# Attention with a routed expert layer on one core: the scatters of a routed group made a job of their own

## The chip, the cores and the metric

The kernel runs on one core of one Trainium2 chip. The metric is the device time of one execution in microseconds (us), median of several runs. Five engines work side by side, each through its own queue of instructions: TensorE (PE in the profile; its weight loads are PEld), VectorE (DVE), ScalarE (ACT), GpSimd (POOL) and SyncE (SP, which here only starts transfers).

## The reference

Everything is float32. `x` has 8 batches of 1024 tokens of 256 values.

```python
def attn(x, Wq, Wk, Wv, Wo):                 # 16 heads of 16
    q, k, v = (einsum('oi,bsi->bso', W, x) split into heads)
    score = where(causal, q @ k.T / 4, -inf)
    return einsum('oi,bsi->bso', Wo, softmax(score) @ v)

def ffn(h, router_weight, router_bias, gate_up_proj, gate_up_bias, down_proj, down_bias):
    scores = softmax(h @ router_weight.T + router_bias)      # 8 experts
    topk_w, topk_idx = top_k(scores, 2)
    gu = h @ gate_up_proj[e] + gate_up_bias[e]               # for every expert e, 2 * 512 wide
    gate, up = minimum(gu[:512], 7), clip(gu[512:], -7, 7)
    down = ((up + 1) * gate * sigmoid(1.702 * gate)) @ down_proj[e] + down_bias[e]
    return sum of the two chosen experts' down, weighted by topk_w

x = x + layernorm(attn(layernorm(x)))
x = x + layernorm(ffn(layernorm(x)))
```

Only the two chosen experts of a token need to be computed. The kernel therefore sorts the tokens by expert on the chip.

## The kernel before, in words

**Two phases.** First attention and routing, then the experts. Between them lies a DRAM buffer `xsd`: one region of rows for each expert, into which every token's normalized row is scattered twice, once for each chosen expert.

**Attention.** The work is cut into 32 units: 8 batches by 4 sets of four heads. A unit has nine steps, and each step has two halves ("half steps", one for each pair of heads), 18 half steps for a unit. While unit u takes its row maxima (matmuls `sa`, L834, reduced on DVE), unit u-1 makes its exponentials and weighted values (matmuls `sb`, L929, exponentials on ACT, L941, causal masks on POOL, L950, matmuls `av`, L970). After the last unit comes one more pass, u = 32, with only the second half of this work.

**Groups and their routing.** Two chunks of 512 tokens leave each batch, 16 "groups" in all, t = 0 to 15. A group's job (`finish`, then `route`) does, one after another: the output projection (matmuls `yps`, L1031), a layer norm and the residual on POOL (L517 the power, L529 the normalization, L1050 the sum), a second layer norm into `xn` (L529 again), four transposes by two (`x2ps`, L1092), the router's logits (`lpsT` L1099, `lps` L1107), softmax and ranks on DVE (L1109 to L1149), a count of the tokens of each expert (`cps`, L1153) and from it each token's row in `xsd` (`slots`). At its end stand eight indirect DMAs of POOL, the scatters of L1194: 128 rows of 258 values each. `finish` of group t waits until group t-2 has transposed its `xn`, and goes on to `route` only when the whole job of group t-2 is done.

**Tables.** After group 11 and after group 15 the job goes on into `table` (L308 to L438 and further): from the counts it works out which expert and which rows each tile of 256 tokens takes. The table after group 11 serves the first 16 tiles. Four tiles' rows are loaded at once by `load_early` (L1283, on SP); these loads read `xsd`, so they have to follow the scatters of groups 0 to 11 both in the program and on the chip.

**Who sets the order.** PE, DVE, ACT and SP execute in the order in which the program was written down. That order is made by a small planner while the kernel is being built. Each job is a generator that yields `piece(pe, dve, act, pool, after)`: the cost of its next piece on each engine and the number of half steps that must pass first. A half step adds its spare time to a credit of each engine (`earn`, at most 0.9 us, POOL 1.3 us). `pump` then takes every piece whose engines have credit left, in the order urgent jobs, the first `due` job, `back` jobs from oldest to newest, and counts one half step. On POOL the order follows the same source order (`in_order`), except that scatters may change places among each other. Where something must be finished, the planner emits pieces without asking for credit: at the end of unit 31 it did so with the oldest `back` job until the table after group 11 stood:

```python
if u == B * NG - 1 and not early:
    while NT - LATE not in known:
        emit(back, back[0])
    load_early()
```

**Experts.** 72 tiles at most, in the order of the tables; `quarter` (matmuls `gu`, L1470), `lower_half` (matmuls `dn`, L1510), an indirect DMA of the results to `ytd` (L1523), and `both`, which adds the two results of each token. The jobs of groups 12 to 15 are carried on beside the first tiles; before tile 14 whatever is left of them is emitted at once (`finish_all`).

## Time and profile before

| | |
|---|---|
| three runs | 2163.42, 2168.82, 2172.29 us, median 2168.82 |
| profiled execution | 2165.1 us, span on the core 2163.0 us |
| busy PE, DVE, ACT, POOL | 2053.6, 1711.3, 1062.6, 1053.1 us |
| the 128 scatters of L1194 on POOL | 129.0 us, mean 1008 ns |
| attention | from the start to about 1380 us of the span |
| experts | from about 1380 us to the end |

PE is busy for 95% of the span. A busy PE share says little about how much it could save, so what is read below is what stands between its matmuls: for each stretch, the time in which PE did nothing, and the instruction of another engine whose end let it go on. In a line of the timeline the columns are the start, the duration, the engine, the line of the kernel, the operation with output and input, and in brackets the idle time of the engine before it with what ended it.

### The profile page before, as it was taken

What the parts mean: (1) busy time and instruction counts of PE and PEld (TensorE: products, weight loads), DVE (VectorE), ACT (ScalarE), POOL (GpSimd) and SP (SyncE); (2) the same over time, 40 slices, a digit from 0 to 9 for tenths busy, and PEclk for the clock granted to TensorE, in tenths of its full rate; (3) what the DMA queues carried; (4) which work ended last, traced back from release to release, by engine and by line L of the source; (5) the groups of instructions that cost most, each with busy time, mean ns of one, the idle gap of its engine ahead of it and who ended that gap; (6) DMA issues with size and microseconds to landing.
All of it is one profiled execution on the core that took longest, in us unless ns stands there. A gap on an engine that the chain in (4) does not pass through costs nothing.

```text
span 2163.0 us, 44648 instructions
## 1 busy us (share of the span) xinstructions
PE 2053.6 (95%) x16205; PEld 1260.0 (58%) x16205; DVE 1711.3 (79%) x4091; ACT 1062.6 (49%) x2072; POOL 1053.1 (49%) x1213
## 2 busy tenths in 40 slices
PE   7899999999999999999999998999999999999995
PEld 3444444444444434434534443688888888888884
DVE  4786886986887887887888788678777888877776
ACT  3566665666666655655655665533123222232222
POOL 3421653472474355455554645455544444444443
PEclk9999999999999999999999999999999999999998
DMA  4101102112112111112111111656877777766774
GB/s 124 24 16 43 35 26 63 34 45 46 42 32 69 20 45 46 49 45 50 47 37 41 44 39 36 209 198 210 263 248 250 268 271 264 261 241 239 271 273 152
DMA packets 147096, 254.85 MB, mean 118 GB/s; under 512 B 21504, under 2 KB 106008, under 8 KB 144952
## 3 DMA queue, kind: packets, MB, share of 16 engines
q1 hardware_dynamic: 133128, 217.01, 32.5%
q0 software_dynamic: 12528, 34.36, 4.3%
q8 instruction: 129, 2.11, 0.4%
q14 instruction: 95, 0.78, 0.1%
q10 hardware_dynamic: 1216, 0.58, 0.1%
HBM read 171.13 MB, written 55.63 MB: 105 GB/s over the span
## 4 chain that ended last, share of the span: by engine, by line
PE 68%; DVE 19%; POOL 6%; issue 4%; ACT 2%; DMA 1%; DVEq 0%; ACTq 0%; POOLq 0%; SPq 0%
PE sa L834 18%; PE gu L1470 14%; PE av L970 10%; PE dn L1510 7%; PE sb L929 5%; PE yps L1031 3%; PE pjk L740 3%; PE pjq L740 3%; PE vps L726 3%; DVE mx L850 3%; DVE sa L844 2%; DVE acc L1585 1%; DVE gate L1479 1%; DVE act L1491 1%; DVE up L1483 1%
## 5 line engine op out<-in xcount | busy, mean ns | idle before, releaser
L941 ACT ACTIVATE pT<-sb 128x512 f32<-128x512 f32 x1134 | 616.3, 595 | 392.3 <-PE sb L929 356.4
L929 PE MATMUL sb<-qP,kP 32*128 32x512 f32 (+3 forms) x3072 | 701.0, 525 | 13.8 <-ACT pT L941 8.9
L834 PE MATMUL sa<-kP,qP 32*128 32x512 f32 (+3 forms) x3072 | 653.7, 525 | 26.0 <-DVE mx L844 13.4
L1470 PE MATMUL gu<-xsT,wg 128*128 128x256 f32 (+1 forms) x2208 | 485.2, 372 | 1.9 <-ACT xsT L1450 1.9
L1470 PEld LDWEIGHTS gu<-xsT,wg 128*128 128x128 f32 x2208 | 407.5, 190 | 56.1 <-ACT xsT L1450 3.4
L850 DVE TENSOR_REDUCE mx<-sa 128x2 f32<-128x1024 f32 x256 | 310.6, 1215 | 116.9 <-PE sb L929 89.7
L950 POOL TENSOR_SCALAR_AFFINE_SELECT pT<-pT 128x512 f32<-128x512 f32 x256 | 164.1, 656 | 466.4 <-ACT pT L941 455.5
L834 PEld LDWEIGHTS sa<-kP,qP 32*128 32x128 f32 x3072 | 226.3, 185 | 248.8 <-issue 100.0
L1481 ACT ACTIVATE sig<-gate 128x256 f32<-128x256 f32 (+1 forms) x276 | 112.8, 409 | 523.9 <-DVE gate L1479 488.2
L970 PE MATMUL av<-pT,vpad 128*32 128x256 f32 (+1 forms) x5120 | 350.2, 370 | 5.0 <-DVE avs L981 3.0
L929 PEld LDWEIGHTS sb<-qP,kP 32*128 32x128 f32 x3072 | 294.1, 185 | 47.1 <-ACT pT L941 18.1
L1486 POOL TENSOR_TENSOR sig<-sig,gate 128x256 f32<-128x256 f32 (+1 forms) x276 | 198.7, 723 | 248.4 <-ACT sig L1481 245.4
L970 PEld LDWEIGHTS av<-pT,vpad 128*32 128x32 f32 x5120 | 117.0, 109 | 292.7 <-issue 235.1
L1510 PE MATMUL dn<-wd,act 128*128 128x256 f32 x1064 | 259.6, 383 | 18.0 <-DVE act L1491 16.8
L1510 PEld LDWEIGHTS dn<-wd,act 128*128 128x128 f32 x1064 | 194.2, 190 | 51.9 <-DVE act L1491 28.7
L1479 DVE TENSOR_SCALAR gate<-gu,bs 128x256 f32<-128x256 f32 (+1 forms) x276 | 128.9, 467 | 106.2 <-PE gu L1470 94.0
L844 DVE CUSTOM_DVE_ANT_0 sa<-sa,cmask 128x512 f32<-128x512 f32 x256 | 177.6, 698 | 39.7 <-PE sb L929 20.3
L1523 POOL DMA_INDIRECT ytd<-ys,places x133 | 133.4, 1003 | 125.2 <-DVE ys L1518 92.7
L1194 POOL DMA_INDIRECT xsd<-xn,slots x128 | 129.0, 1008 | 63.7 <-DVE xn L1190 34.3
L1491 DVE SCALAR_TENSOR_TENSOR act<-up,sig 128x256 f32<-128x256 f32 (+1 forms) x276 | 124.5, 451 | 26.6 <-POOL sig L1486 26.6
L869 ACT COPY edge<-sa 128x512 f32<-128x512 f32 x192 | 112.9, 588 | 41.2 <-DVE mx L859 20.2
L888 DVE TENSOR_REDUCE mx<-edge 128x8 f32<-128x1024 f32 x96 | 115.6, 1205 | 18.1 <-POOL edge L883 18.1
(243 smaller groups left out, 2335.0 us busy)
## 6 DMA issues: line engine op xcount, KB each, us to landing
wg<-_L_ffn_gate_up_proj_dram SPq DMA_DIRECT2D x69, 1024.0 KB
wd<-in_L_ffn_down_proj_dram SPq DMA_DIRECT2D x69, 512.0 KB
xs<-xsd SPq DMA_DIRECT2D x60, 258.0 KB
yy<-ytd SPq DMA_DIRECT2D x15, 1024.0 KB
bs<-biasd SPq DMA_DIRECT2D x69, 132.0 KB
x<-in_L_attn_x_dram SPq DMA_DIRECT2D x16, 512.0 KB
aT<-avn SPq DMA_DIRECT2D x256, 32.0 KB
x1d<-y SPq DMA_DIRECT2D x16, 512.0 KB
```

The costliest lines, as they stand in the source:

```text
L834: nc.tensor.matmul(ps[:, hh, ds(at, w)], lhsT=qP[r, ts(i, P)], rhs=kP[r, ds(c * QC, w)], start=True, stop=True,)
L844: nc.vector.tensor_tensor_reduce(out=ps[:, hh, :], in0=ps[:, hh, :], in1=cmask, scale=1.0, scalar=NEG, op0=ALU.add, op1=ALU.max, accum_out ...
L850: nc.vector.tensor_reduce(mx[:, heads, i, 2:3], ps, AX.X, ALU.max)
L929: nc.tensor.matmul(banks[hh][:, ds(at, QC - off)], lhsT=kP[r, ts(j, P)], rhs=qP[r, ds(c * QC + off, QC - off)], start=True, stop=True,)
L941: nc.scalar.activation(pT[:, 2 * pair + hh, :], banks[hh], AF.Exp)
L950: in_order(nc.gpsimd.affine_select(out=d, in_=d, compare_op=ALU.is_ge, fill=0.0, base=0, pattern=[[0, HG], [1, P]], channel_multiplier=-1,))
L970: nc.tensor.matmul(av[ds(hh * HS, HS), ds(off + a - at, z - a)], lhsT=vp[:, j, ds((g * HG + hh) * VS, HS)], rhs=pT[:, hh, a:z],  start=c n ...
L1470: nc.tensor.matmul(ps[:, half, :w], lhsT=wg[:, kt, ds(half * FF + f * P, P)], rhs=xT[:, kt, :], start=(kt == 0), stop=(kt == KT - 1),)
L1479: nc.vector.tensor_scalar(gt, ps[:, 0, :w], bs[:, f : f + 1], LIMIT, ALU.add, ALU.min)
L1486: in_order(nc.gpsimd.tensor_tensor(sg, sg, gt, ALU.mult))
L1491: nc.vector.scalar_tensor_tensor(act[:, f, :w], up, 1.0 - LIMIT, sg, ALU.max, ALU.mult)
L1510: nc.tensor.matmul(pss[n][:, 0, :], lhsT=act[:, f, ts(n, P)], rhs=wd[:, f, :], start=(f == 0), stop=(f == FT - 1),)
```

## The change

The eight scatters at the end of `route` become a generator of their own, `scatter_rows`. For groups 0 to 14 it is started as a new `back` job, with 3 half steps before its first scatter and 4 before each further one, where there was 1 before. For the last group it is run through on the spot. The job of a group then goes on at once to its end, or to its table. Two waits are added: `route` of group t first waits until every scatter of group t-2 has been emitted, since `xn` has two buffers, and the early loads wait until the scatters of groups 0 to 11 have been emitted (`early_known`). At the end of unit 31 the planner now emits one piece of every `back` job in turn, until both the table after group 11 and all those scatters stand.

```diff
+        def scatter_rows(t, xn, last):
+
+            rest = 0 if last else 4
+            for r in range(TOPK):
+                for n in range(NTB):
+                    yield piece(pool=1.1, after=rest if n or r else 1 if last else 3)
+                    put = nc.gpsimd.indirect_dma_start(
...
+        def scattered(t):
+            return t in puts and (t >= NT - TN or puts[t].done)
+
         def route(t, x1, last):
 
+            while t > 1 and not scattered(t - 2):
+                yield piece(after=1)
             xn = ap2.tile([P, NTB, XD], F32, tag="xn2", name=f"xn2_{t}")
...
-            for r in range(TOPK):
-                for n in range(NTB):
-                    yield piece(pool=1.1, after=0 if last and (n or r) else 1)
-                    put = nc.gpsimd.indirect_dma_start(
...
+            puts[t] = scatter_rows(t, xn, last)
+            if last:
+                yield from puts[t]
+            else:
+                puts[t] = start(back, puts[t])
...
+        def early_known():
+            return NT - LATE in known and all(scattered(t) for t in range(NT - LATE))
...
-                    if u == B * NG - 1 and not early and NT - LATE in known:
+                    if u == B * NG - 1 and not early and early_known():
                         load_early()
...
                 if u == B * NG - 1 and not early:
-                    while NT - LATE not in known:
-                        emit(back, back[0])
+                    while not early_known():
+                        for job in list(back):
+                            emit(back, job)
                     load_early()
```

More of the change, by code (lines that the diff above doesn't have):

```diff
@@ L1072, in normed @@
             yield piece(after=1)
+        puts = {}
+        def scatter_rows(t, xn, last):
[4 more added lines that the diff above has]
+                    put = nc.gpsimd.indirect_dma_start(
+                        out=xs_dram[:, :],
+                        out_offset=bass.IndirectOffsetOnAxis(ap=slots[:, t, r, n : n + 1], axis=0),
+                        in_=xn[:, n, :], in_offset=None,
+                    )
+                    in_order(put, scatter=True)
+                    apart(put, "xs")
+        def scattered(t):
+            return t in puts and (t >= NT - TN or puts[t].done)
         def route(t, x1, last):
+            while t > 1 and not scattered(t - 2):
+                yield piece(after=1)
             xn = ap2.tile([P, NTB, XD], F32, tag="xn2", name=f"xn2_{t}")
@@ L1190, in route @@
             nc.vector.tensor_reduce(xn[:, :, D + 1], first_of, AX.X, ALU.add)
-            for r in range(TOPK):
-                for n in range(NTB):
-                    yield piece(pool=1.1, after=0 if last and (n or r) else 1)
-                    put = nc.gpsimd.indirect_dma_start(
-                        out=xs_dram[:, :],
-                        out_offset=bass.IndirectOffsetOnAxis(ap=slots[:, t, r, n : n + 1], axis=0),
-                        in_=xn[:, n, :], in_offset=None,
-                    )
-                    in_order(put, scatter=True)
-                    apart(put, "xs")
+            puts[t] = scatter_rows(t, xn, last)
[3 more added lines that the diff above has]
+                puts[t] = start(back, puts[t])
             if nth == NT - 1:
```

## The prediction

> **What bounds the kernel now.** I read the page's head with the engines' shares first, then the busy time by stretch (start and end, length, then busy us and count of PE, PEld, DVE, ACT and POOL, granted clock, DMA share, GB/s), then PE's timeline where attention ends.

> ```profile
> span 2163.0 us, 44648 instructions
> PE 2053.6 (95%) x16205; PEld 1260.0 (58%) x16205; DVE 1711.3 (79%) x4091; ACT 1062.6 (49%) x2072; POOL 1053.1 (49%) x1213
> ```

> ```profile
> 100.00:1300.00 1200.00, 1160.93 (x11248) 546.62 (x11244) 975.99 (x2177) 745.47 (x1395) 588.42 (x647) 0.99 0.17 42
> 1345.00:1357.00 12.00, 7.68 (x51) 3.12 (x47) 5.22 (x23) 3.46 (x7) 3.90 (x5) 0.73 0.22 52
> ```

> PE sets the time. From 100 to 1300 us it is idle for only 1200 - 1160.93 = 39.1 us. The one place where it waits for long is the end of unit 31, where the granted clock falls to 0.73:

> ```profile
> 1300.99 0.38 PE L1153 MATMUL cps<-chosen,before 128*128 128x32 f32 x2 [2.35 <-DVE chosen L1149]
> ...
> 1346.32 0.64 PE L970 MATMUL av<-pT,vpad 128*32 128x256 f32 x8
> 1346.89 0.39 PE L371 MATMUL firstps<-seg,before 128*128 128x2 f32 x2
> 1350.33 0.62 PE L417 MATMUL tabps<-two,ones 128*128 128x144 f32 x2 [3.06 <-DVE two L414]
> 1352.21 0.57 PE L438 MATMUL takenps<-each,ones 128*128 128x8 f32 x2 [1.26 <-DVE each L435]
> 1352.71 2.09 PE L929 MATMUL sb<-qP,kP 32*128 32x512 f32 x8
> ...
> 1361.31 1.14 PE L929 MATMUL sb<-qP,kP 32*128 32x512 f32 x8
> ```

> The reader is to see three things: the rest of the table is emitted there at once, and PE leaves the `av` before it at about 1346.96 and takes its next main work at 1352.71, **5.75 us** later; what stands in PE's queue waits for DVE and nothing behind it goes ahead; the eight `sb` after the idle time take 2.09 us, later 1.14.

> **What the change does to the order.** The planner works at build time, so its choices are known. A group's count and table no longer wait for its own scatters. But `route` of group t waits for those of group t-2, and these now take 3 + 7 x 4 = 31 half steps where they took 8. Counted in the planner's half steps, 18 to a unit: group 6 waits at that point from 354 to 390, and its scatters begin at 440 where they began at 402. The lag stays (groups 7, 8, 9: 473, 528, 548, were 427, 474, 499). Unit 31 ends at 576. Before, group 10 was done by 548 and group 11 needed only four more pieces of its table. Now group 10 has only its normalized `xn`, group 11 has not begun its second layer norm, and 3 + 8 + 8 scatters of groups 9, 10, 11 are left. Since `early_known` wants all of it, 24 rows of matmuls of groups 10 to 13 stand between the last `av` of unit 31 and the first `sb` of u = 32, in a chain through every engine; before there were 3 rows. The step that must be right is the length of this chain.

> **The chain, from the rows of this profile.** The prices:

> ```profile
> L517 POOL TENSOR_TENSOR rstd<-ve,nhalf_seg 128x4 f32<-128x4 f32 x48 | 50.4, 1050 | 155.9 <-DVE ve L512 155.7
> L529 POOL TENSOR_SCALAR xn<-y,mv,rstd 128x256 f32<-128x256 f32 x52 | 63.2, 1224 | 1.2
> L1050 POOL TENSOR_TENSOR y<-y,x 128x256 f32<-128x256 f32 x56 | 41.1, 734 | 3.1
> L1194 POOL DMA_INDIRECT xsd<-xn,slots x128 | 129.0, 1008 | 63.7 <-DVE xn L1190 34.3 <-issue 28.4 <-DVE shift L1062 0.6
> L508 DVE BATCH_NORM_STATS2 st<-y 128x6 f32<-128x256 f32 x128 | 52.5, 410 | 0.0
> L509 DVE BATCH_NORM_AGGREGATE mv<-st 128x2 f32<-128x6 f32 x192 | 34.9, 182 | 6.6
> ```

> Zero is the end of the last `av`. Rows of DVE, ACT and PE that are not shown are those of group 12's routing in the timeline from 1338 to 1375.

> (1) POOL ends group 10's `xn`: 1 us, since its `ve` stands behind the reduction that came at about 1341 and one power and four L529 take 6 us. (2) PE: `x2ps` 0.66 twice, `yps` of group 12 1.92 twice, `lpsT` 0.62, `lps` 0.48, ACT's copy 0.3 between: to 7.7. (3) DVE, before group 11's `ve` may go: small logit and softmax rows (0.15 to 0.2 each) 1.2, eight pairs of L508 and L509 at 0.59 that are mixed in 4.7, `gt` and `ge` 1.0: to 14.6. (4) POOL: two L517 2.1, then group 11's four L529 with two L529 and one L1050 of group 12 between them, 6 x 1.22 + 0.73, 0.4 between instructions: to 25.2. (5) PE for group 11 as in (2), 5.7 to the end of `lpsT` at full clock and some 2 more because the idle time lowers it, as at 1352.71, then the copy and `lps` 0.8: to 33.7. (6) DVE to group 13's `ve`, four pairs and the same small rows: to 38.4; PE is idle again. (7) POOL has emptied its queue by 35.4, group 10's first five scatters included, and waited; from 38.4 on, in its order: L517, 3 scatters, 4 L529 and 4 L1050 of group 13, a scatter, L517, then 4 scatters mixed with group 12's four L529: 2 x 1.05 + 8 x 1.01 + 8 x 1.22 + 4 x 0.73 = 22.9, about 2 between them: to 63.4. Meanwhile DVE and PE bring group 11 to its table (54 to 55), so POOL ends later. (8) PE: two `x2ps`, ACT's copies of 0.58, `lpsT` of group 12, at half clock: to **67.6**. Against 5.75 that is +61.8.

> **What comes back.** The work moved into the chain no longer stands in the half steps: six `x2ps` 3.5, four `yps` 7.7, three `lpsT` 1.5, two each of `lps` and `cps` 2.1, `segps` 0.8: -15.6. There it stood on the bound engine, so I take it whole; the lower bound on the saving, nothing, is where DVE sets the half steps instead (the waits of `sa` for `mx`, 13.4 us in all). The restart at 1352.71 is slow until about 1356.6; after the new chain PE has just worked at half clock for 4 us, so its 2 us go: -2. Sum: 61.8 - 15.6 - 2 = **+44**.

> Costed at nothing: the scatters' own count (128 either way); the tests, which are done at build time; the masks of u = 32 behind the last three scatters in POOL's queue (they end at 66.5, before ACT has made the first exponential for them); the early loads on SP, which now also wait for those scatters. They started at 1352.39 and the first tile's transposes at 1380.34, so 28 us cover them; behind them on SP stand the transfers of `aT` and the weights, ahead of them only group 12's store of `x1d`, ready at 30. Without that cover each microsecond of landing counts in full. The last table's end now falls to the emission before tile 14 (half step 753, was 748); its `two` is made four half steps earlier, so PE has no new wait; 0 to 2 us. In attention, fewer scatters lie close together: PE's waits for POOL from 150 to 1300 us are 0.5 us in the list of waits, so nothing.

> Bounds. No row shows such a chain, and POOL's spans are rough. If POOL's part were hidden, group 11's table would end it: 56.8 - 5.75 - 15.6 - 2 = +33. If nothing of the moved work came back: +60. I take +44, which uses each row once. The steady part may move by 10 either way, a quarter of its 39.1 us.

> [...]

> **Rivals.** *The table ends the chain, not POOL*: for it, POOL's rows are rough and 24 of them make 25 us; against it, each has its own measured mean. +33: 2198. *The loads wait*: the scatters are issued up to 66.5, and if their landing uses up the 28 us of cover, the first tiles stand still; a scatter's landing is seen only in the last chain (3.02 and 2.71 us for `ytd`), which speaks against it. 10 to 25 us on top, 2225. *No change*: the attention phase gains what the break costs. With the forecast's chain it would have to win 44 us, more than the 39.1 it is idle; with the table as the chain's end 33 of them. 2165. *Faster*: the evenly spread scatters unblock POOL so that PE never waits from 100 to 1300 us, 39.1 gained, and POOL runs the break so fast that the table ends it: 33 - 39.1 = -6, 2159; it decides only above 33 us gained. The waits name DVE's `mx` and ACT's `pT`, not POOL, so it is unlikely. That it doesn't do what it says is not a case of its own: the order shows that counts and tables do still wait, through the next groups, and that is the forecast.

> **Numbers.** The profiled execution took 2165.1 us (span 2163.0 and 2.1 around it), 3.7 below the median of the runs. 2165.1 + 44 = 2209; put between the two bases, **2211**. Chances: forecast 0.70, table 0.12, loads 0.11, no change 0.04, faster 0.03. The range takes the table with 8 us won elsewhere and the loads' middle with 10 lost: 2190 to 2236. About 0.5% is what a measurement of this kernel can tell from no change. Faster 0.03, same 0.04, slower 0.93.

> **What would show it.** In PE's timeline `x2ps` of group 10 directly after unit 31's last `sa` and `av`; an idle time of about 10 us before the first `cps` and 6 before the next `x2ps`, ended by DVE `chosen` and POOL `xn`; some 66 us to the next `sb`; a granted clock below 0.8 there; POOL's last scatters just before the masks; experts of the same length. Wrong would be a break below 40 us, an attention phase shorter by more than 25 us ahead of it, or a wait for transfers at the first tile.

## The result

| | before | after |
|---|---|---|
| median of six runs each | 2168.95 us | 2187.16 us (2183.75 to 2191.7) |
| profiled execution, span | 2165.1, 2163.0 us | 2184.7, 2183.0 us |

The ratio of the times is 1.0088, with a 95% interval of 1.0067 to 1.0108: slower, but by 18 to 20 us and not by 44. The time lies just under the range of the prediction, which begins at 2190.

The changed kernel has a break where it was predicted, and it is about as long. The head of its page, and its windows for most of attention and for the break (start and end, length, busy us and count of PE, PEld, DVE, ACT and POOL, granted clock, DMA share, GB/s):

```profile
span 2183.0 us, 44671 instructions
PE 2049.4 (94%) x16205; PEld 1261.5 (58%) x16205; DVE 1712.6 (78%) x4091; ACT 1062.9 (49%) x2072; POOL 1053.9 (48%) x1213
```

```profile
100.00:1300.00 1200.00, 1173.40 (x11563) 549.06 (x11558) 995.68 (x2167) 765.41 (x1429) 568.78 (x629) 1.00 0.17 41
1300.00:1363.00 63.00, 23.39 (x142) 16.77 (x142) 32.52 (x138) 7.73 (x16) 50.31 (x52) 0.63 0.14 53
```

From 100 to 1300 us PE starts 11563 matmuls where it started 11248 before: attention runs faster. That was not in the forecast. Then comes the break, in which POOL is the busiest engine, 50.31 of 63 us, and PE works 23.39 us at a granted clock of 0.63. PE's timeline inside it, with what ended each idle time:

```profile
1307.01 0.33 PE L1128 MATMUL lps<-ident,lgT 128*128 128x128 f32 x1 [0.39 <-ACT lgT L1125]
1315.56 0.61 PE L1174 MATMUL cps<-chosen,before 128*128 128x32 f32 x2 [8.23 <-DVE chosen L1170]
...
1330.30 0.33 PE L1128 MATMUL lps<-ident,lgT 128*128 128x128 f32 x1 [0.39 <-ACT lgT L1125]
1337.18 0.60 PE L1174 MATMUL cps<-chosen,before 128*128 128x32 f32 x2 [6.55 <-DVE chosen L1170]
...
1348.45 0.98 PE L363 MATMUL segps<-ident,new 128*128 128x1 f32 x4 [10.23 <-DVE new L356]
...
1360.12 1.33 PE L1113 MATMUL x2ps<-ident,xn 128*128 128x128 f32 x5 [2.05 <-POOL xn L529]
...
1362.71 1.84 PE L929 MATMUL sb<-qP,kP 32*128 32x512 f32 x8
```

The reader is to see the chain of the forecast in its order: group 10's logits and ranks, group 11's, the table (`segps`), and at the end the four `x2ps` of group 12, each waiting for the next `xn` that POOL makes between its scatters.

Cut at marks that both traces have (the end of the last `av` of unit 31, the first `sb` of u = 32, the first `gu`, the `gu` that opens the seventeenth tile, the end), the 20.0 us come from:

| stretch | before | after | difference | forecast |
|---|---|---|---|---|
| start to the last `av` of unit 31 | 1346.96 | 1300.89 | -46.1 | -15.6 |
| the break, to the first `sb` of u = 32 | 5.75 | 61.82 | +56.1 | +61.8 |
| to the first `gu` | 28.97 | 27.36 | -1.6 | -2 |
| the first sixteen tiles | 193.55 | 204.35 | +10.8 | 0 to 2 |
| the rest | 587.81 | 588.58 | +0.8 | 0 |

Two steps of the forecast are right to within some us, and two are not: attention gained 30 us more than the forecast gave back for the work that was moved out of it, and the first tiles lost 9 to 11 us more than forecast.

**Where attention gains.** The gain grows from unit 16 on: 1.6 us at the start of unit 16, 15.3 at unit 20, 29.9 at unit 27, 41.4 at unit 31. In the trace of before there are six places where PE, ACT and DVE all stand idle at once for about 2 us, with no wait on POOL; after five of them the granted clock is 0.5 for 3.4 us. One of them, in the timeline of before with all engines:

```profile
994.34 1.08 ACT L941 ACTIVATE pT<-sb 128x512 f32<-128x512 f32 x2 [0.52 <-PE sb L929]
994.39 1.10 POOL L1194 DMA_INDIRECT xsd<-xn,slots  x1 [4.75 <-DVE xn L1190]
...
998.32 0.96 POOL L1194 DMA_INDIRECT xsd<-xn,slots  x1 [0.30 <-issue]
1000.43 1.23 DVE L850 TENSOR_REDUCE mx<-sa 128x2 f32<-128x1024 f32 x1 [4.13 <-PE sa L834]
1000.53 1.08 ACT L941 ACTIVATE pT<-sb 128x512 f32<-128x512 f32 x2 [5.11 <-PE sa L834]
...
1001.18 1.89 PE L929 MATMUL sb<-qP,kP 32*128 32x512 f32 x4 [1.86 <-ACT pT L941]
```

Four scatters start 1.3 us apart, at 994.4 to 998.3. ACT and DVE had nothing from PE for 5.11 and 4.13 us. PE's own rows, whose ends are modelled, show only 1.86 us of idle time there. The moments at which PE counts up the semaphore that others wait for are also in the trace: none between 994.36 and 1000.41, and DVE, which had waited for `sa`, starts at 1000.43. The counts also stand still from 775.68 (3.5 us), 822.63 (5.5), 949.72 (3.5), 1121.29 (3.5) and 1168.13 (6.0), each at a run of four or five scatters of groups 4 to 9, and from 648.64 (3.9), at a run of three. The three long ones, 5.5 to 6.0 us, are the clear ones: pauses of 3.0 to 3.4 us also occur where no scatter stands (784.99, 796.76, 969.02, 1142.55). In the changed kernel the scatters of these groups lie some 3 to 30 us apart, or in twos, but for a run of three and one of five. Three scatters of group 6 after the change (before, five of its eight stood in one run):

```profile
1009.17 1.10 POOL L1082 DMA_INDIRECT xsd<-xn,slots  x1 [0.18 <-issue]
...
1016.47 0.98 POOL L1082 DMA_INDIRECT xsd<-xn,slots  x1 [0.16 <-issue]
1017.75 0.96 POOL L1082 DMA_INDIRECT xsd<-xn,slots  x1 [0.30 <-issue]
```

Of pauses of 3.5 us or more two are left in its attention (850.9, at the run of five, and 1135.4, at two scatters).

### The profile page after: what moved, and what is told of

Read it like the earlier page. It is cut to its first block, busy times and chain, and to the rows that moved or that the text cites. A ratio compares the mean times of both kernels' runs of the same rounds, so it can differ in the third digit from the quotient of the medians.

```text
span 2183.0 us, 44671 instructions
## 1 busy us (share of the span) xinstructions
PE 2049.4 (94%) x16205; PEld 1261.5 (58%) x16205; DVE 1712.6 (78%) x4091; ACT 1062.9 (49%) x2072; POOL 1053.9 (48%) x1213
## 4 chain that ended last, share of the span: by engine, by line
PE 64%; DVE 21%; POOL 8%; issue 4%; ACT 2%; DMA 1%; SPq 0%; DVEq 0%; POOLq 0%; ACTq 0%
PE sa L834 16%; PE gu L1490 13%; PE av L970 10%; PE dn L1530 7%; PE sb L929 5%; DVE mx L850 3%; PE pjq L740 3%; PE yps L1031 3%; PE vps L726 3%; PE pjk L740 3%; DVE sa L844 2%; DVE acc L1605 1%; POOL ytd L1543 1%; DVE mx L888 1%; DVE gate L1499 1%
## 5 line engine op out<-in xcount | busy, mean ns | idle before, releaser
L929 PE MATMUL sb<-qP,kP 32*128 32x512 f32 (+3 forms) x3072 | 693.7, 524 | 0.3 <-ACT pT L941 0.3
L970 PE MATMUL av<-pT,vpad 128*32 128x256 f32 (+1 forms) x5120 | 347.4, 368 | 7.2 <-DVE avs L981 6.0
L929 PEld LDWEIGHTS sb<-qP,kP 32*128 32x128 f32 x3072 | 292.1, 185 | 27.5 <-ACT pT L941 6.6
L970 PEld LDWEIGHTS av<-pT,vpad 128*32 128x32 f32 x5120 | 116.6, 108 | 296.3 <-issue 239.0
L1499 DVE TENSOR_SCALAR gate<-gu,bs 128x256 f32<-128x256 f32 (+1 forms) x276 | 129.0, 467 | 114.1 <-PE gu L1490 102.5
L869 ACT COPY edge<-sa 128x512 f32<-128x512 f32 x192 | 113.1, 589 | 46.0 <-DVE mx L859 23.8
L1503 DVE TENSOR_SCALAR up<-gu,bs 128x256 f32<-128x256 f32 (+1 forms) x276 | 128.0, 464 | 0.0
```

What stands on the lines that cost most here:

```text
L929: nc.tensor.matmul(banks[hh][:, ds(at, QC - off)], lhsT=kP[r, ts(j, P)], rhs=qP[r, ds(c * QC + off, QC - off)], start=True, stop=True,)
L970: nc.tensor.matmul(av[ds(hh * HS, HS), ds(off + a - at, z - a)], lhsT=vp[:, j, ds((g * HG + hh) * VS, HS)], rhs=pT[:, hh, a:z],  start=c n ...
L1499: nc.vector.tensor_scalar(gt, ps[:, 0, :w], bs[:, f : f + 1], LIMIT, ALU.add, ALU.min)
```

## The experiments

Theory of the **runs**: PE stands still while several scatters are issued one directly behind the other, and the change gains by drawing them apart. Theory of the **order**: attention is shorter only because work was pushed out of it, and close scatters are harmless. All times are us, and each ratio is to runs of the kernel before that were taken together with that experiment; "attention" is from the first `sa` of unit 2 to the last `av` of unit 31 (1251.0 before, 1203.8 after), "break" and "tiles" as in the table above.

### One: a small operation between the scatters of before

```diff
                     in_order(put, scatter=True)
                     apart(put, "xs")
+                    if t < NT - LATE and (n, r) != (NTB - 1, TOPK - 1):
+                        in_order(nc.gpsimd.tensor_tensor(spacer, ones[:, :NTB], nhalf, ALU.pow))
```

> The kernel before, with one more small POOL instruction (a power on 128x4) between the scatters of groups 0 to 11, so that two scatters of a group never start 1.3 us apart. PE, DVE, ACT and SP keep their order. Theory 'runs': in before, PE stands still for 2 to 4 us where four or more scatters follow each other 1.3 us apart, and often loses 1.7 us more to the lowered clock; without such runs attention is 20 to 28 us shorter, 2141 to 2152 us, even though POOL has some 85 us more work. Theory 'order': attention became shorter in the changed kernel because the routing's pieces on PE and DVE fall into other half steps, and the spacing on POOL is nothing; then 2169 us or, with the added POOL work, up to 2180.

Measured: 2163.23, ratio to before 0.9968 (0.9951 to 0.9986). Attention 1241.8, break 5.6, tiles 195.5. The scatters now start 2.3 us apart, no two of them directly behind each other, and the time falls by 6 us although POOL got 84 more instructions; but `sa` waits for `mx` with single waits of 3.39 and 3.26 us at 1281.7 and 1315.9 (23.8 us for `mx` in all from 100 to 1345). Attention is 9.2 shorter where the theory of the runs had 20 to 28, so the time is too mixed to size them. The counts are clearer: in the 1.27 us from the start of the third and of the fourth scatter of such a row of scatters PE counts 1.89 and 1.88 times (2.26 on the mean of attention); in before, where they start 1.27 us apart, 0.22 and 0.62. With 2.3 us between starts PE goes on.

### Two: the changed kernel with runs of four

```diff
+            held = []
...
+                    held.append((r, n))
+                    if not last and len(held) < NTB:
+                        continue
+                    for hr, hn in held:
...
```

> The changed kernel, with the scatters held back until four are due and then issued back to back; PE, DVE, ACT and SP keep their order exactly. Theory 'runs': PE stands still again at most of the two runs of each group, 15 to 25 us more in attention, 2200 to 2212 us. Theory 'order': 2187 us, within 4.

Measured: 2232.37, ratio 1.0295 (1.0262 to 1.0327). Attention 1236.1, break 63.6, tiles 214.5. DVE, ACT and SP have the order of the changed kernel to the instruction, PE too but for `sa` and `sb` that run side by side, and it is 45 us slower, of which attention 32.3. This alone rules out the order as the only cause; the size was underestimated.

### Three: the separate job, but one half step between scatters

```diff
-            rest = 0 if last else 4
+            rest = 0 if last else 1
```

> The changed kernel with 1 half step between two scatters instead of 4 (first one after 3). The scatters are still a job of their own; 8 scatters take 10 half steps, the routing of group t-2 is no longer late, and nothing is forced at the end of unit 31. The break theory says the 62 us break is gone. Theory 'runs': the scatters follow each other as closely as before, so attention is as long as before: 2163 to 2175 us in all. Theory 'order', or a gain from the separate job itself: attention keeps 15 to 30 us of what the changed kernel gained: 2140 to 2155.

Measured: 2199.86, ratio 1.0148 (1.0111 to 1.0185). There is no break, yet attention takes 1262.4, 11 more than before, and the tiles 214.4. Ten runs of four to eight scatters stand in attention here, most of them of six. So the job of its own gains nothing in attention; the distance does.

### Four: at the break only what is needed

```diff
+                        needed = [*finishes[: NT - LATE], *puts.values()]
                         for job in list(back):
-                            emit(back, job)
+                            if any(job is j for j in needed):
+                                emit(back, job)
```

> The changed kernel, but in the forced emission at the end of unit 31 only the jobs of groups 0 to 11 and the scatters are carried on, not those of groups 12 and 13. Theory of the prediction (POOL's in-order work for groups 12 and 13 sets the second half of the break): the break falls from 62 to 42 to 48 us, some 8 us of matmuls return to later places, 2173 to 2181 us in all. Rival (the chain of group 11 through DVE and PE to its table sets it alone): break above 55 us, 2184 or more.

Measured: 2178.82, ratio 1.0051 (1.0035 to 1.0068). The break is 35.3, shorter than expected, but the tiles take 218.7: the 26 us won come back as 14 in the tiles and 6 before the first `gu`. So the pieces of groups 12 and 13, which the changed kernel drags into the break, make up 26 of its 62 us, and most of that work has to be done later anyway.

### Five, six and seven: two together, four together, two half steps

```diff
-            rest = 0 if last else 4
+            rest = 0 if last else 2
...
-                    yield piece(pool=1.1, after=rest if n or r else 1 if last else 3)
+                    yield piece(pool=1.1, after=1 if last and not (n or r) else 0 if last else 3 if not (n or r) else 0 if n % 2 else rest)
```

The sixth has `rest = 4` and `0 if n else rest` in that place, the seventh only the first of the two changes.

> The changed kernel with two scatters together and two half steps between such pairs, where it had one and four. The planner's order then needs no forced emission at the end of unit 31 (the scatters of group 11 are emitted by half step 566 of 576). Theory of the runs (PE stands still for 2 us and more where four or more scatters start 1.3 us apart; single ones and pairs do no harm): the time from the start of unit 2 to the last av, 1251 us before, becomes 1220 to 1235 and the break stays at 5 to 7 us; the first sixteen tiles take 195 to 215; in all 2140 to 2158, faster than both kernels. Theory of the order (attention was shorter only because work was pushed out of it into the break): with no break nothing is pushed out, attention takes 1248 to 1262, in all 2165 to 2185.

> The changed kernel with four scatters together and four half steps before the next four; as in the kernel of two together, next to nothing is forced at the end of unit 31 and the break stays at 5 to 10 us. It is that kernel with runs of four for runs of two. Theory of the runs: halts of about 2 us with half clock after them come back, one or two for each group, and the time from unit 2 to the last av is 1245 to 1270; in all 2165 to 2195, at least 15 us over the kernel with pairs. Theory of the order: within 8 us of the kernel with pairs.

> The changed kernel with two half steps between single scatters instead of four. The planner forces 19 pieces at the end of unit 31 instead of 72 and more, group 11's scatters among them. Theory of the runs: attention 1215 to 1235 us from unit 2 to the last av, the break 15 to 30, in all 2150 to 2168. Theory of the order: what the break gains attention gives back, in all 2170 to 2187.

Measured: the pairs 2196.44, ratio 1.0125 (1.0098 to 1.0152), attention 1256.5, no break, tiles 213.5. The fours 2167.88, 0.9988 (0.997 to 1.0007), attention 1243.3, break 6.6, tiles 200.4. Two half steps 2159.12, **0.9952 (0.9937 to 0.9968)**, attention 1217.2, break 28.2, tiles 194.6.

By its number the fifth goes against the theory of the runs, and the sixth as well. The trace shows why: what the planner puts two half steps apart does not stay apart on the chip. POOL took up the scatters in its queue only after the work ahead of them, which waited for its input, and then issued them all at once. After a wait of 2.48 us for `pT`, two masks and an `edge`, three of the "pairs" of group 2 started as one run of six (608.8, 610.1, 611.3, 612.6, 613.9, 615.1); the "fours" started partly as twos. The theory has to be put to the starts that the trace shows, not to the plan. Counted so (this count was made after the results; a run is a row of starts at most 1.5 us apart, 2 in the kernel with runs of four), over the kernels that change only the scatters:

| kernel | scatters that are third or later in a run, up to the last `av` | attention |
|---|---|---|
| after (with the 15.6 moved out added back) | 4 | 1219.4 |
| two half steps | 12 | 1217.2 |
| two, then one (the twelfth) | 20 | 1231.8 |
| fours without a break | 20 | 1243.3 |
| before | 21 | 1251.0 |
| pairs | 34 | 1256.5 |
| runs of four (with 15.6 added) | 38 | 1251.7 |
| one half step | 39 | 1262.4 |

More such scatters go with a longer attention, but not in strict order: kernels with 20 and 21 lie 19 us apart. The kernels in which 15.6 was not added lack a few matmuls of before in this stretch too (at most eight `x2ps`, sixteen `lpsT`, four `cps` and six `segps`), some 2 to 3 us by the prediction's prices.

The seventh kernel beats both, before by 0.5%: half the distance gives up little of attention's gain, and more than half of the break goes. Its break in PE's timeline:

```profile
1329.41 0.98 PE L363 MATMUL segps<-ident,new 128*128 128x1 f32 x4 [10.37 <-DVE new L356]
...
1342.25 0.48 PE L1113 MATMUL x2ps<-ident,xn 128*128 128x128 f32 x1 [3.26 <-POOL xn L529]
...
1346.18 2.18 PE L929 MATMUL sb<-qP,kP 32*128 32x512 f32 x8
```

Group 10's chain is no longer in it. One wait for the table is left, and then POOL's alternation of `xn` and scatters as in the changed kernel.

### Eight: groups 12 to 15 scatter inside their own job

```diff
-            if last:
+            if t >= NT - LATE:
                 yield from puts[t]
```

(and one half step between their scatters, as before the change)

> The changed kernel, but groups 12 to 15 run their scatters inside the group's job, one each half step, as before the change; attention and the break are untouched. If the 10.8 us that the first sixteen tiles take longer come from the later jobs of groups 12 to 15, they take 193 to 198 us again and the whole 2172 to 2179. If they come from where the break leaves those jobs (their state at the start of the experts), nothing changes: 203 to 206 and 2183 to 2189.

Measured: 2184.54, ratio 1.0069 (1.0047 to 1.009); tiles 202.5. The first reading falls: the later jobs of these groups make the tiles longer by 2 us at most. What stands in PE's way there is read from its list of waits over these tiles, after:

```profile
PE dn L1530 <- DVE act L1511: 4.5, 6, 1.6
PE x2ps L1113 <- ACT xn L1068: 3.2, 5, 2.2
PE yps L1031 <- DMA aT<-avn: 2.7, 1, 2.7
PE segps L363 <- DVE new L354: 1.6, 1, 1.6
PE cps L1174 <- DVE chosen L1170: 1.6, 1, 1.6
```

and before:

```profile
PE dn L1510 <- DVE act L1491: 5.2, 6, 1.8
PE x2ps L1092 <- issue: 0.4, 1, 0.4
PE cps L1153 <- DVE chosen L1149: 0.2, 1, 0.2
```

Both traces have the same matmuls in these tiles. PE is idle 15.4 us after and 7.5 before, and 3.4 us at half clock, 1.7 lost, come on top: 9.6 of the 10.8. The waits that are new are those of the last groups' chain (`x2ps`, `yps`, `segps`, `cps`: 9.1 us against 0.6): its pieces now fall so that PE comes to them before their input is there. Which shift of the planner does it was not singled out.

### Nine, ten, thirteen and fourteen: what in a run of scatters holds PE

The changed kernel, and behind the eighth scatter of groups 2 to 9 five scatters more into a buffer of their own. They take POOL 6.3 us at each of the eight places (5.8 with 16 rows, 6.5 for the powers).

```diff
+            for n in range(EXTRA if 2 <= t < 10 else 0):
+                more = nc.gpsimd.indirect_dma_start(
+                    out=more_dram[:, :],
+                    out_offset=bass.IndirectOffsetOnAxis(ap=slots[:, t, n // NTB, n % NTB : n % NTB + 1], axis=0),
+                    in_=xn[:, n % NTB, :WIDE], in_offset=None,
+                )
```

The tenth has `WIDE` = 16 for 258, the thirteenth six powers in their place, the fourteenth 16 of the 128 rows (`slots[:16, ...]`, `xn[:16, ...]`).

> The changed kernel with five more scatters of the same rows directly behind the eighth scatter of groups 2 to 9, into a buffer of their own that nothing reads (work added, none left out); the order of everything else is untouched. POOL gets 8 runs of six, some 42 us more of scatters. Theory of the runs, by their transfers: eight halts of 2 us and more with half clock after them, attention from unit 2 to the last av 1218 to 1240 us where the changed kernel has 1203.8, in all 2200 to 2222. If close scatters do no harm and only POOL's time counts: no such halts, attention 1204 to 1212, in all 2185 to 2195.

> As the kernel with five more scatters behind groups 2 to 9, but each moves 16 of the 258 values of a row: the same instructions on POOL and as many rows, a sixteenth of the bytes. If the halts come from the bytes that the transfers move, they are gone: attention 1204 to 1212 us, in all 2185 to 2195. If they come from the issue of the scatters on POOL or from the number of rows, they stay: attention and time within 6 us of the kernel with whole rows.

> The changed kernel with six more powers of 128 x 4 values on POOL (1.04 us each in its rows) where the kernel with extra rows has five more scatters: the same stretch of POOL's queue is taken (6.3 us), at the same eight places, without a scatter. Theory of the scatters (PE gets almost nothing done while a run of scatters is being issued, whatever they carry): powers do no such harm, attention 1204 to 1214 us, in all 2185 to 2197. If the extra scatters did harm only by holding up the masks that stand behind them on POOL: the same as there, attention 1240 to 1255, in all 2225 to 2240.

> As the kernel with five extra scatters behind groups 2 to 9, but each scatters 16 whole rows instead of 128. If PE is held by the instruction's issue on POOL, whatever it moves: attention 1240 to 1255 us, in all 2225 to 2240, as with 128 rows. If it is held by the number of rows: at most a fifth of the 43 us that the 128 rows cost is left, attention 1204 to 1213, in all 2185 to 2196. The scatters themselves may become shorter on POOL; then the loss is set against their own time.

| | time, ratio to before | attention | six places up to the start of unit 31, each |
|---|---|---|---|
| after | 2187.16, 1.0088 | 1203.8 | |
| five scatters, whole rows | 2234.46, 1.0327 (1.0302 to 1.0353) | 1246.6 | +5.9 |
| five scatters, 16 of 258 values | 2235.96, 1.0333 (1.0308 to 1.0358) | 1250.1 | +6.5 |
| five scatters, 16 of 128 rows | 2254.0, 1.0431 (1.039 to 1.0473) | 1257.0 | +7.7 |
| six powers | 2203.72, 1.0173 (1.013 to 1.0217) | 1216.2 | +0.8 |

The last column is the time from the start of unit 2 to that of unit 31, less that of the changed kernel (1169.5), over six. The three kernels with scatters keep to the theory of the runs, two of them above its ranges; the powers lie 2 us above theirs in attention and 7 in all. The same place, first POOL and ACT with five scatters more:

```profile
682.04 0.96 POOL L1092 DMA_INDIRECT mored<-xn,slots  x1 [0.30 <-issue]
...
688.37 0.96 POOL L1084 DMA_INDIRECT xsd<-xn,slots  x1 [0.30 <-issue]
```

```profile
690.88 1.09 ACT L943 ACTIVATE pT<-sb 128x512 f32<-128x512 f32 x2 [7.57 <-remote]
```

and ACT with powers from 682.47 to 688.95:

```profile
682.92 1.09 ACT L942 ACTIVATE pT<-sb 128x512 f32<-128x512 f32 x2 [0.53 <-PE sb L930]
685.09 1.08 ACT L942 ACTIVATE pT<-sb 128x512 f32<-128x512 f32 x2 [1.08 <-PE sb L930]
```

Beside the powers ACT goes on as ever; beside the scatters it gets nothing for 7.57 us. So at these six places it is not POOL's queue, and not a mask that waits in it: the powers hold that for as long. At the seventh, in unit 31, PE did wait for a mask behind the powers (3.80 us for `pT`, then 3.27 for `mx`); that is most of what the powers cost attention beyond the six places. It is not the bytes, since a sixteenth of them does as much harm, and not the number of rows, since an eighth of them does more. PE's count of its semaphore shows it directly. It moves 2.27 times per 1.27 us on the mean of attention before. In the 1.27 us from the start of the first scatter of a run it is 1.70, of the second 1.06, of the third 0.22, of the fourth 0.62; of the fifth, in the four runs that have one, 1.75 again. With five scatters more it is 0.33, 0.62, 0.62, 0.29 and 0 for the third to the seventh; during the powers 2.2; with runs of four (the second kernel) 0.89 and 0.39 for the third and fourth. From the third scatter on PE loses most of these runs. Whether the first two do harm was not tried by itself.

### Eleven and twelve: can the break go as well?

The eleventh joins two half steps with the fourth's "only what is needed"; the twelfth has two half steps for groups 0 to 7 and one from group 8 on.

```diff
-            rest = 0 if last else 4
+            rest = 0 if last else (2 if t < 8 else 1)
```

> The changed kernel with two half steps between scatters, and at the end of unit 31 only the jobs of groups 0 to 11 and the scatters are emitted out of turn; 15 pieces are forced there. Theory of the runs and of the break as the only two terms: attention as with two half steps alone, 1214 to 1222 us; the break 12 to 20 where it was 28.2; the first sixteen tiles 195 to 205, since group 12 is further behind; in all 2146 to 2160. If group 12's work comes back in full at the tiles: 2158 to 2168.

> The changed kernel with two half steps between scatters for groups 0 to 7 and one from group 8 on; nothing of weight is forced at the end of unit 31, so the break goes. Theory of the runs: groups 8 to 11 have runs of four to six again, each with a halt, and what the break gives (22 us) is lost in part: attention 1232 to 1252 us, break 0 to 7, tiles 195 to 214, in all 2148 to 2180, and the halts stand at groups 8 to 11 alone (and where groups 4 and 5 had them with two half steps). Theory of the order: attention stays at 1217 to 1225, in all 2135 to 2148.

Measured: 2168.59, ratio 1.0019 (1.0008 to 1.003), attention 1215.6, break 15.3, tiles 222.1; and 2169.49, 1.0027 (1.0012 to 1.0041), attention 1231.8, no break, tiles 221.6. The breaks shrink as expected, and the tiles take 27 us more than with two half steps alone. In both, the tiles have group 12's 8 `yps` and 16 `lpsT` in addition, and PE is idle 25 us there, where it was 8. What is not emitted in the break is late before tile 14. The eleventh lies just over its second case, in which group 12's work comes back. The twelfth lies in the range of the theory of the runs in all, and at its lower edge in attention (group 9's scatters are a run of eight, and PE's gaps of 1.59 and 1.22 us with half clock stand behind it), but for other tiles than expected.

### Fifteen: before once more

> The kernel before, unchanged, in a second profiled execution. If the gaps of about 2 us in PE belong to the order of the program, they stand at the same six places within 1 us, 779 to 1173; if they are chance of one execution, elsewhere or not at all.

Measured: 2164.28. The idle times that PE's rows show stand at only three of the six places (1.77 us at 824.7, 1.07 at 997.5, 0.96 at 1169.9; all places are 1 to 4 us earlier). The counts of the semaphore stand still at all six: from 775.0, 819.7, 948.2, 992.5, 1117.3 and 1164.9, for 3.3, 6.0, 3.2, 5.3, 3.3 and 3.8 us. Only those of 6.0 and 5.3 stand out from the pauses without scatters, which in this execution reach 3.8 (at 1295.5). So the halts at these two places clearly belong to the program; how long a halt is, and how much of it is shown as idle time of PE, does not repeat.

## Why the prediction was wrong

- **The step that failed**: "In attention, fewer scatters lie close together: PE's waits for POOL from 150 to 1300 us are 0.5 us in the list of waits, so nothing." So the sum had -15.6 for attention, and -46.1 was measured. About 30 of it is the distance, if the moved work gave its 15.6; with runs of four put back (the second kernel) 32.3 of it are lost again. The list of waits could not show it: PE does not wait for POOL at these halts; it stands still beside it, and the list names "issue" (2.07 us at 781.37) or ACT's `pT` (1.86 at 1001.18). Six of the idle times in the 39.1 us were 2 us long and stood where scatters stood, and PE's rows with modelled ends hid the larger part of the long halts. So the 39.1 us were no ceiling either: between 100 and 1300 us the idle time shown fell only to 26.6.
- **Luck**: the total misses by 24 us although attention alone missed by 30 and the break by 6, both the same way. The 10.8 us of the first tiles, which were not foreseen either, went the other way; without them the time would have been some 9 us over before.
- **The break**: 61.8 us where 67.6 was forecast, +56.1 against +61.8 before the 2 us at the restart. The chain held link by link: `lps` of group 11 ended at 29.7 us (forecast 33.7), `tabps` began at 52.0 (54 to 55), and POOL ended it with `xn` between scatters, not the table. Of the 6 us that it is short, 4 were won up to `lps` of group 11 and 1.6 in the last link, from POOL's last `xn` to `sb` (2.6 for 4.2). The 24 rows of POOL that the prediction names are 22 in its own list; its sum of 22.9 is that of the 22.
- **The clock in the break**: half for 17.1 and 30.7 us, from 1309.6 and 1333.5. Both times it went down while PE stood idle, 2.2 and 2.8 us after the end of its last matmul, and came up again during a close row of matmuls, at 1326.6 in eight `yps` and at 1364.2 in the eight `sb`. In before the clock was at half from 1350.5 to 1357.4; the prediction read 1352.71 to about 1356.6 off PE's rows. The forecast took half clock only for parts of its steps (5) and (8).
- **What comes back**: 15.6 for the work that was moved. Between the start of unit 2 and the last `av`, the trace after has 32 `yps`, 23 `x2ps` and 48 `lpsT` fewer, which is that list. That it gave back its full price was not measured by itself. The restart gave 1.6 (2 forecast).
- **The first tiles**: 0 to 2 us forecast, 10.8 measured. The forecast followed one instruction (`two`, ready four half steps earlier) and not the chain of groups 12 to 15 ahead of it; its cause is known only as far as the eighth experiment goes.
- **The rival "faster"** had the right place and the wrong mechanism: it let spread scatters "unblock POOL", found no wait that named POOL, and fell to 0.03. The gain that it needed, more than 33 us, was nearly there (30 besides the moved work), but the break did not become shorter by the table ending it. "An attention phase shorter by more than 25 us" was named as what would make the prediction wrong, and it is what did.

## What to carry to other kernels

Look for the moments in which several engines stand idle together, and for what another engine does at that moment, even where no wait names it: a list of waits shows who was released by whom, not what slows an engine down. Here five indirect scatters more in a run, about 6 us of POOL, cost PE 5.9 to 7.7 us, so issue them apart (2.3 us from start to start was enough for PE's counts); and read the starts in the trace, since POOL's queue, held for 2.48 us by a wait, here issued six scatters in a bunch that the planner had spread as pairs. When drawing work apart makes it late, price what then has to be finished in one go: here four half steps won 46 us in attention, 16 of them, by the forecast's prices, work that was only moved, and lost 67 in the break and the tiles; two half steps kept most of the gain at half of the break.
